# Layer 1 of a two-layer network: folded convolution weights replaced by one projection and shifted rows through DRAM

## The chip, the cores and the metric

The kernel runs on one core of a Trainium2 chip. The metric is the device time of one execution in microseconds (us); the time of a kernel is the median of its runs. One core has a matrix engine (TensorE, PE), a vector engine (VectorE, DVE), an activation engine (ScalarE, ACT), a general engine (GpSimd, POOL) and SyncE (SP), which here issues all the transfers.

## The reference

4096 tokens of 256 channels pass through two layers, each a mixing step and a feed-forward step, with adaptive layer norms around them. Layer 0 is attention with 16 heads and a mixture of experts. Layer 1 is a gated delta rule with four heads of 64 and a "fractal mixer", then a quantized linear step. Only layer 1's first half changes:

```python
def short_conv(x, w):                 # w: 4 taps per channel
    y = sum((xp[:, t:t + l, :] * w[:, t] for t in range(K)))   # xp: 3 zero rows ahead
    return y * jax.nn.sigmoid(y)
# q, k, v = short_conv(x @ W, conv) for each of Wq, Wk, Wv
def fractal_mixer(x, conv_w):
    out = 2.0 * x
    for i in range(4):                # shifted back by 1, 2, 4, 8 rows
        out = out + x_shift * conv_w[i, :, 0] + x * conv_w[i, :, 1]
```

After that, q and k are turned by rotary angles and normed. Within each chunk of 32 tokens a lower triangular matrix, made of k's products and beta, is inverted, and a scan over the chunks carries a state S of 64x64 for each head.

## The kernel before, in words

The 4096 tokens are 32 tiles of 128, or 8 blocks of four tiles. Layer 0's attention runs first, then its mixture of experts (`mixture`, L764), block by block, with layer 1's weights made meanwhile in small pieces, then `layer1` (L1155).

**Fronts.** `fronts` (L1290) is a generator that goes over the blocks. `project` (L1355) transposes the normed block (`nxn`) to channels on partitions (`hT`), splits it in a high and a low part (`hh`, so that three rounded products stand for an fp32 one) and makes the gates. `convolve` (L1409) makes q, k, v and the mixer of one tile directly from `hh`: the projection and its four taps were folded into one set of weights, `taps`, by `taps_in_weights` (L806), which writes them to a DRAM buffer `td`; eight loads of 864 KB bring them in before layer 1. A tile takes 24 matmuls of 128x512 for q and k (four taps, two halves of the channels, three products), 24 of 384 or 256 columns for v and mixer, and four fp32 products with `far` for the mixer's shifts by 4 and 8 rows; the shifts themselves are offsets in `hh`, which keeps eight columns of the block before. ScalarE applies Silu, VectorE turns q and k (`by`, `rot`, L1454 to L1472) and norms them. Some pieces later `by_channel` (L1534) brings them to channels, and `products` (L1551) makes L, which goes through DRAM (`dL`, then `Ls`, L1577), so that all matrices of a block lie on partitions. `solve` (L1581) inverts them in 31 "columns" of two VectorE instructions each, which `solving` (L1629) lets out a few at a time, and the inverse goes through DRAM into `U` (L1619).

**Backs.** `backs` (L1635) goes over the tiles: `from_inverse` (L1657) multiplies U with v and k; `scan` (L1673) has four chunks, each with products of w and S, VectorE's `ut` (L1695), products of ut and k, and VectorE's new `S` (L1718); `weights`, `outputs` and the linear step follow, and the result is stored.

**Order.** `layer1` runs the fronts alone until the first block is solved, then LEAD more front pieces, and then after each yield of the backs RATE front pieces (LEAD 21, RATE 48/60; 60 yields and 48 pieces make a block of four tiles). `later(n, f)` in `stream` puts a function off by n pieces, and so decides where by_channel, products and the first columns stand. TensorE's and VectorE's instructions are pinned in the order of the program (`mm` L139, `tp`, `dv`, `mma`); the rest is placed by a scheduler. SP issues transfers in order[...]. Results of TensorE turn through four PSUM buffers, `pf` (`f` in the profile); the scan's are `w`.

Of the kernel before, what the change touches and what calls it, by code (L numbers as in the profile page):

```python
# [7 lines left out]
F32 = mybir.dt.float32  # L8
# [9 lines left out]
P = 128  # L18
S = 4096
# [22 lines left out]
LEAD = 21  # L42
RATE = 48 / 60
KEPT = 9

A_N = 4 * 2 * 2 * 512
B_W = {3: 384, 2: 384, 1: 384, 0: 256}
B_AT = {3: A_N, 2: A_N + 4 * 384, 1: A_N + 8 * 384, 0: A_N + 12 * 384}  # L50
W_N = A_N + 12 * 384 + 4 * 256
# [51 lines left out]
class _Net:  # L103
# [660 lines left out]
    def mixture(self):  # L764
        nc, tc = self.nc, self.tc
        with ExitStack() as c:
# [18 lines left out]
            taps = self.taps_in_weights()  # L785
            for b in range(NB):
# [4 lines left out]
                for n, f in enumerate(self.experts(b)):  # L791
                    f()
                    while ahead and slots[-len(ahead)] <= n:
                        ahead.pop(0)()
                    if b and n in (1, 4, 8) and taps:
                        taps.pop(0)()
                nc.sync.dma_start(out=self.xd[b], in_=self.xs.pop(b))
                if b == NB - 2:

                    self.right.close()  # L800
                    self.taps = self.t(
                        self.ctx.enter_context(tc.tile_pool(name="taps", bufs=1, side="right")),
                        [P, W_N],
                        "taps",
                        F32R,
                    )  # L806
                    for at in range(0, W_N, 1728):
                        nc.sync.dma_start(
                            out=self.taps[:, at : at + 1728].bitcast(F32), in_=self.td[:, at : at + 1728]
                        )  # L810
# [6 lines left out]
    def taps_in_weights(self):  # L817


        nc, a, dp = self.nc, self.a, self.dram  # L820
        self.td = td = self.t(dp, [P, W_N], "td")
        taps = self.t(self.mw, [P, 3 * C, 4], "taps")
        wide = self.t(self.mw, [P, 2, 3 * C], "wqkv")
        for i, name in enumerate("qkv"):
            cols = slice(C * i, C * i + C)
            nc.sync.dma_start(
                out=taps[:, cols, :].rearrange("p c t -> p (c t)"),
                in_=a["L1_attn_conv_" + name].rearrange("c t -> (c t)").partition_broadcast(P),
            )
            nc.sync.dma_start(  # L830
                out=wide[:, :, cols], in_=a["L1_attn_W" + name].rearrange("(k p) n -> p k n", p=P)
            )
        fw = self.t(self.mw, [P, 4, 2, 2], "fw")
# [5 lines left out]
        own = self.t(self.mw, [P, 2], "own")  # L839
        self.dv(nc.vector.tensor_tensor(own, fw[:, 0, :, 1], fw[:, 1, :, 1], ALU.add))  # L840
        for i in (2, 3):
            self.dv(nc.vector.tensor_tensor(own, own, fw[:, i, :, 1], ALU.add))
        self.dv(nc.vector.tensor_scalar(own, own, 2.0, None, ALU.add))
        pieces = []

        def kept(full, outs):

            _, n, width = full.shape
            cut = self.t(self.ms, [P, 512], "cut")[:, 0 : n * width].rearrange("p (n w) -> p n w", n=n)
            self.dv(nc.vector.tensor_scalar(cut.bitcast(I32), full.bitcast(I32), HIGH, None, ALU.bitwise_and))  # L850
            self.dv(nc.gpsimd.tensor_tensor(full, full, cut, ALU.subtract))
            for half, of in enumerate((cut, full)):
                for i in range(n):
                    nc.sync.dma_start(out=td[:, outs[half][i] : outs[half][i] + width], in_=of[:, i, :])

        def queries_keys(t, k):
            full = self.t(self.ms, [P, 512], "full").unsqueeze(1)
            self.dv(
                nc.vector.tensor_tensor(full[:, 0], wide[:, k, 0:512], taps[:, 0:512, t], ALU.mult)
            )  # L860
            kept(full, [[512 * (4 * t + 2 * half + k)] for half in range(2)])

        def values(t):
            full = self.t(self.ms, [P, 512], "full").rearrange("p (k n) -> p k n", k=2)
            by = taps[:, 512:768, t].unsqueeze(1).to_broadcast([P, 2, C])
            self.dv(nc.vector.tensor_tensor(full, wide[:, :, 512:768], by, ALU.mult))

            outs = [
                [B_AT[t] + B_W[t] * (2 * half + k) + (P if k == 0 and t else 0) for k in range(2)]
                for half in range(2)  # L870
            ]
            kept(full, outs)

        def mixer(t):
            full = self.t(self.ms, [P, 512], "full")[:, 0:C].rearrange("p (k n) -> p k n", k=2)
            for k in range(2):
                col = own[:, k : k + 1] if t == 3 else fw[:, 2 - t, k, 0:1]
                self.dv(nc.vector.tensor_scalar(full[:, k], self.ident, col, None, ALU.mult))
            kept(full, [[B_AT[t] + B_W[t] * (2 * half + k) + C * k for k in range(2)] for half in range(2)])

        for t in range(4):
            pieces += [lambda t=t, k=k: queries_keys(t, k) for k in range(2)]
            pieces.append(lambda t=t: values(t))
            if t:
                pieces.append(lambda t=t: mixer(t))
        return pieces
# [268 lines left out]
    def layer1(self):  # L1155
        nc, tc, a = self.nc, self.tc, self.a
        with ExitStack() as c:
# [9 lines left out]
            self.hT = self.t(wp, [P, 2, 8 + 512], "hT")  # L1167
            self.hh = self.t(wp, [P, 2, 2, 8 + 512], "hh", F32R)
            nc.gpsimd.memset(self.hT[:, :, 0:8], 0.0)
            nc.gpsimd.memset(self.hh[:, :, :, 0:8].bitcast(F32), 0.0)  # L1170
# [6 lines left out]
            self.tiles, self.blocks, self.solved, self.columns = {}, {}, 0, []  # L1177

            front, back = self.stream(self.fronts), self.stream(self.backs)
            def alone(b):  # L1180
                while self.solved < b + 1:
                    next(front, None)
                    self.solving()
# [37 lines left out]
    def layer1_weights(self):  # L1221
# [18 lines left out]
        fw = self.t(wp, [P, 2, 2], "fw")  # L1240
        for i in range(2):
            nc.sync.dma_start(
                out=fw[:, i, :],
                in_=a["L1_attn_frac_conv_w"][2 + i, :, 0].rearrange("(k p) -> p k", p=P),
            )
        w["far"] = self.t(wp, [P, 2, 2, P], "far")
        for i in range(2):
            for k in range(2):
                nc.vector.tensor_scalar(w["far"][:, i, k, :], self.ident, fw[:, i, k : k + 1], None, ALU.mult)


# [38 lines left out]
    def fronts(self, later):  # L1290
        nc = self.nc
        for f in self.norm_block(0):
            f()
        for b in range(NB):
            yield from self.project(b, later)
            for s in range(4):
                if s == 2 and b + 1 < NB:
                    self.load_block(b + 1)
                    for k, f in enumerate(self.norm_block(b + 1)):
                        later(4 + 2 * k, f, quiet=True)  # L1300
                yield from self.convolve(b, s, later)
                n = 4 * b + s
                later(4, lambda n=n: self.by_channel(n))
                later(6, lambda n=n: self.products(n, later))
# [611 lines left out]
```

## Time and profile before

| what | value |
|---|---|
| runs | 3083.62, 3067.89, 3074.98 us, median 3074.98 us |
| profiled execution | 3099.04 us, its span 3097.2 us |
| mean granted TensorE clock | 0.924 |
| layer 0's attention and mixture | to about 2156 us of the span |
| first matmul with `U` | 2312.6 us |
| fronts and scan together | 2312 to 2943 us |
| scan alone | 2943 to 3097 us |

A line of the chain or the timeline has the start and the length in us, then the engine, the tile or the instruction, and the number of records (xN); in square brackets stands how long the engine was idle before and what ended that. A line of stretches has each engine's busy time and number of records, then the granted clock of TensorE (1.00 is full), the busy share of the transfer engines and GB/s. An fp32 matmul leaves two records. The row PEclk on the page shows the granted clock in 40 equal slices, in tenths.

### The profile page before, as it was taken

How to read it: one execution, taken by the hardware profiler on the slowest of the kernel's cores; microseconds unless marked ns; L12 is line 12 of the kernel's file. 1: busy time of each engine (PE TensorE's matmuls, PEld its weight loads, DVE VectorE, ACT ScalarE, POOL GpSimd, SP SyncE). 2: the span in 40 equal slices, each digit the busy share in tenths (PEclk: the TensorE clock that was granted, in tenths of full speed). 3: DMA queues.
4: the chain of work that ended last, by engine and by line, in shares of the span. 5: the costliest groups of instructions: out<-in, count | busy, mean ns of one | idle time of the engine just before them, and what ended most of it. 6: DMA issues, size and time to landing. Idle time of an engine off the chain costs nothing.

```text
span 3097.2 us, 59936 instructions
## 1 busy us (share of the span) xinstructions
PE 2857.7 (92%) x24005; PEld 1674.7 (54%) x24092; DVE 2255.0 (73%) x3905; ACT 1735.3 (56%) x3684; POOL 477.8 (15%) x708
## 2 busy tenths in 40 slices
PE   7899999999999999999999989998878998899877
PEld 4453444444444444444443477776766776677655
DVE  6685889888888988889875177766357667766765
ACT  3335777777777787787887422221444444444321
POOL 3231000000000000000000022221322333333212
PEclk9896999999999999999999599999889998999955
DMA  5453000030000300001000111113111111111100
GB/s 183 139 181 56 12 12 7 12 52 7 12 12 7 52 7 12 12 19 44 7 2 2 48 38 51 55 45 117 38 20 21 21 23 30 29 22 21 22 17 11
DMA packets 174230, 114.30 MB, mean 37 GB/s; under 512 B 122432, under 2 KB 145216, under 8 KB 173376
## 3 DMA queue, kind: packets, MB, share of 16 engines
q1 hardware_dynamic: 173808, 110.41, 13.6%
q8 instruction: 190, 3.11, 0.4%
q14 instruction: 88, 0.72, 0.1%
q0 software_dynamic: 144, 0.07, 0.0%
HBM read 63.62 MB, written 44.89 MB: 35 GB/s over the span
## 4 chain that ended last, share of the span: by engine, by line
PE 66%; DVE 23%; ACT 5%; issue 3%; DMA 2%; POOL 1%; SPq 1%; DVEq 0%; POOLq 0%; ACTq 0%
PE o L142 17%; PE e L142 13%; PE f L142 10%; DVE mx L611 9%; PE m L142 8%; PE b L1352 6%; PE a L1352 4%; PE w L142 2%; PE ps L1352 2%; DVE step L1599 2%; PE f L1352 2%; ACT e L729 2%; DVE T L1606 1%; DVE by L1454 1%; PE f L1343 1%
## 5 line engine op out<-in xcount | busy, mean ns | idle before, releaser
L729 ACT ACTIVATE e<-e 128x512 f32<-128x512 f32 (+1 forms) x2176 | 1153.2, 583 | 346.6 <-PE e L142 313.3
L611 DVE TENSOR_REDUCE mx<-m 128x2 f32<-128x1024 f32 (+3 forms) x1088 | 1201.7, 1128 | 148.0 <-PE m L142 136.1
L142 PE MATMUL o<-e,vall 128*32 128x256 f32 (+2 forms) x9216 | 710.4, 384 | 6.1 <-ACT ot L706 5.2
L142 PE MATMUL e<-q,kt 50*128 50x512 f32 (+3 forms) x2688 | 581.8, 448 | 1.3 <-ACT e L729 1.2
L142 PE MATMUL m<-kt,q 48*128 48x512 f32 (+3 forms) x2688 | 479.4, 375 | 24.2 <-DVE mx L621 9.0
L142 PEld LDWEIGHTS e<-q,kt 50*128 50x128 f32 x2688 | 253.9, 190 | 448.7 <-issue 263.3
L142 PE MATMUL f<-taps,hh 128*128 128x512 f32 (+2 forms) x1536 | 386.0, 394 | 0.3 <-POOL hh L1374 0.3
L142 PEld LDWEIGHTS o<-e,vall 128*32 128x32 f32 x9216 | 194.0, 110 | 332.5 <-issue 307.5
L142 PEld LDWEIGHTS f<-taps,hh 128*128 128x128 f32 x1536 | 278.3, 201 | 40.8 <-POOL hh L1374 0.7
L142 PEld LDWEIGHTS m<-kt,q 48*128 48x128 f32 x2688 | 249.8, 189 | 90.4 <-issue 38.6
L1352 PE MATMUL b<-w,hid 128*128 128x512 f32 x768 | 204.1, 410 | 0.0
L914 POOL TENSOR_TENSOR full<-full,ga 128x512 f32<-128x512 f32 (+1 forms) x2 | 2.0, 1000 | 1122.2 <-DMA full<-in_L_attn_bo_dram 1109.5
L1690 ACT ACTIVATE gs<-S,gm 128x64 f32<-128x64 f32 x256 | 76.5, 342 | 158.1 <-DVE S L1718 158.0
L1352 PEld LDWEIGHTS b<-w,hid 128*128 128x128 f32 x768 | 146.6, 193 | 33.9 <-ACT hid L893 0.3
L1139 DVE SCALAR_TENSOR_TENSOR x<-b,wd,x 128x256 f32<-128x256 f32 x256 | 123.4, 482 | 55.2 <-PE b L1352 48.0
L621 DVE TENSOR_REDUCE mx<-m 128x8 f32<-128x1024 f32 x64 | 78.4, 1225 | 64.3 <-PE m L142 64.2
L1718 DVE TENSOR_TENSOR S<-gs,w 128x128 f32<-128x128 f32 x128 | 36.6, 286 | 118.4 <-PE w L142 117.9
L142 PE MATMUL w<-S,uw 64*32 64x64 f32 x1024 | 60.4, 245 | 58.5 <-DVE S L1718 57.6
L1695 DVE TENSOR_TENSOR ut<-uw,w 32x256 f32<-32x256 f32 x128 | 53.3, 417 | 76.5 <-PE w L142 74.9
L1352 PE MATMUL a<-hs,kt 128*128 128x512 f32 x384 | 103.6, 408 | 1.3 <-DVE hid L1089 1.3
L1599 DVE TENSOR_TENSOR step<-T,Ls 128x126 f32<-128x126 f32 (+22 forms) x248 | 81.2, 327 | 24.8 <-ACT T L1589 19.4
L142 PE MATMUL w<-ut,kk 32*64 32x64 f32 x1024 | 64.3, 250 | 26.6 <-DVE ut L1695 26.6
(288 smaller groups left out, 3167.1 us busy)
## 6 DMA issues: line engine op xcount, KB each, us to landing
q<-qd SPq DMA_DIRECT2D x128, 96.0 KB
kt<-kd SPq DMA_DIRECT2D x12, 768.0 KB
kd<-high SPq DMA_DIRECT2D x32, 256.0 KB
qd<-high SPq DMA_DIRECT2D x32, 256.0 KB
x<-in_L_attn_x_dram SPq DMA_DIRECT2D x15, 512.0 KB
taps<-td SPq DMA_DIRECT2D x8, 864.0 KB
kd<-full SPq DMA_DIRECT2D x16, 256.0 KB
qd<-full SPq DMA_DIRECT2D x16, 256.0 KB
```

The costliest lines, as they stand in the source:

```text
L142: self.nc.tensor.matmul(out, lhsT, rhs, start=start, stop=True, skip_group_check=skip)
L611: nc.vector.tensor_reduce(mx[:, 2 * pair : 2 * pair + 2, s, col], ps[:, :, at : at + w], AX.X, ALU.max)
L621: nc.vector.tensor_reduce(mx[:, 2 * pair : 2 * pair + 2, :, 0], ps.rearrange("p h (s k) -> p h s k", k=P), AX.X, ALU.max,)
L729: nc.scalar.activation(e[:, 0:at], ps[:, 0:at], AF.Exp)
L1139: nc.vector.scalar_tensor_tensor(x, ps[:, e, :], wd[:, s, n : n + 1], x, ALU.mult, ALU.add)
L1343: self.tc.keep_in_program_order(self.nc.tensor.transpose(out, src, ident))
L1352: self.nc.tensor.matmul(out, lhsT, rhs, start=(k == 0), stop=(k == n - 1))
L1454: nc.vector.tensor_tensor(by[z].rearrange("p (i h) f two -> p i (h f) two", i=2), qk.rearrange("p i h (f two) -> p i (h f) two", two=2), c ...
L1599: nc.vector.tensor_tensor(step[:, 0:m, 0:n], T[:, 0:m, j].unsqueeze(2).to_broadcast([P, m, n]), Ls[:, j + 1 : 32, j].unsqueeze(1).to_broad ...
L1690: nc.scalar.activation(gs[:, pair, :], state[:, pair, :], AF.Identity, scale=gm[:, pair, c : c + 1])
L1695: nc.vector.tensor_tensor(ut[rows].rearrange("p (a b) d -> p a b d", b=2), u[rows].rearrange("p (a b) d -> p a b d", b=2), pw[rows, :, 0:1 ...
L1718: nc.vector.tensor_tensor(self.state, gs, pw[:, 0, 128:256].rearrange("p (a d) -> p a d", d=64), ALU.add)
```

## The change

The projections of q, k and v are computed once per block, by channel (channels on partitions, tokens along the row), and written to DRAM buffers of 256 rows with a head of three zeros (eight for the mixer, whose rows are `hT`). `load_shift` brings half a block (256 tokens) of one kind back as a tile of 1 MB: four transfers, each of 32 partitions and 8 groups of 1 KB, and each read from a different shift. Partition 32 i + c of group g so holds channel 32 g + c shifted by i (by 2^i for the mixer). `convolve` multiplies this by stationary matrices of 128x32 with the taps on four diagonals, one for each group of 32 channels: four products stand side by side in four column groups. The mixer also gets its unshifted part by a 128x128 product. Silu is applied by channel, and `mix` transposes the results back to tokens for each tile and goes on as `convolve` did before. Three buffers of shift tiles turn: once a convolution has been issued, the load of the tile three further on is.

The folding of taps, `td`, its loads, `far` and the kept columns of `hh` go. The weights of the front are made in eight pieces in the last block of the mixture. The order is set anew: front pieces per block 35 rather than 48, LEAD 10, shorter delays for keys, products and the first column, more columns at a time, four buffers for `gm`.

```diff
-LEAD = 21
-RATE = 48 / 60
-KEPT = 9
+LEAD = 10
+RATE = 35 / 60
+KEPT = 10
+KINDS = ("q", "k", "v", "m")
...
-            taps = self.taps_in_weights()
+            self.taps_by_row()
+            pieces = []
...
-                    if b and n in (1, 4, 8) and taps:
-                        taps.pop(0)()
+                    if n % 2 and pieces:
+                        pieces.pop(0)()
...
-                    for at in range(0, W_N, 1728):
...
+                    pieces = self.front_weights()
...
-    def taps_in_weights(self):
...
+    def front_weights(self):
...
+        self.rows_d = {}
+        zero = self.t(fp, [P, 2, 8], "zero")
+        nc.gpsimd.memset(zero, 0.0)
+        for kind in KINDS:
+            ahead = 8 if kind == "m" else 3
+            self.rows_d[kind] = d = self.t(self.dram, [C, ahead + S], "d" + kind)
+            nc.sync.dma_start(
+                out=d[:, 0:ahead].rearrange("(k p) n -> p k n", p=P), in_=zero[:, :, 0:ahead]
+            )
...
+        def projection(i, name):
+            full = self.t(self.ms, [P, 512], "full")
+            wide = full.rearrange("p (k n) -> p k n", k=2)
+            nc.sync.dma_start(out=wide, in_=a["L1_attn_W" + name].rearrange("(k p) n -> p k n", p=P))
+            cut = self.t(self.ms, [P, 512], "cut")
             self.dv(nc.vector.tensor_scalar(cut.bitcast(I32), full.bitcast(I32), HIGH, None, ALU.bitwise_and))
...
+            cols = slice(C * i, C * i + C)
+            two = cut.rearrange("p (k n) -> p k n", k=2)
+            nc.scalar.copy(wqkv[:, 0, :, cols], two)
+            self.dv(nc.gpsimd.tensor_tensor(wqkv[:, 1, :, cols], wide, two, ALU.subtract))
+        def taps(kind):
+            for t in range(4):
+                at = slice(32 * t, 32 * t + 32)
+                row = self.rows_of[kind][at, :, 0 if kind == "m" else t].rearrange("p (g c) -> p g c", c=32)
+                eye = self.ident[at, at].unsqueeze(1).to_broadcast([32, 8, 32])
+                self.dv(nc.vector.tensor_tensor(cw[kind][at], row, eye, ALU.mult))
...
-                    self.solving()
+                    self.solving(3)
...
-        nc = self.nc
         for f in self.norm_block(0):
             f()
+        for k in range(2):
+            yield from self.by_channels(0, k)
+        yield from self.gates(0, later)
+        yield from self.project(0)
         for b in range(NB):
-            yield from self.project(b, later)
+            more = b + 1 < NB
             for s in range(4):
-                if s == 2 and b + 1 < NB:
+                n = 4 * b + s
+                parts = self.mix(b, s, later)
+                for kinds in ("qk", "vm"):
+                    if s in (0, 2):
+                        for kind in kinds:
+                            self.convolve(b, s // 2, kind)
+                            yield None
+                    next(parts)
+                    yield None
+                later(3, lambda n=n: self.keys_by_channel(n))
+                later(4, lambda n=n: self.products(n, later))
+                if s == 1 and more:
                     self.load_block(b + 1)
-                    for k, f in enumerate(self.norm_block(b + 1)):
-                        later(4 + 2 * k, f, quiet=True)
-                yield from self.convolve(b, s, later)
-                n = 4 * b + s
-                later(4, lambda n=n: self.by_channel(n))
-                later(6, lambda n=n: self.products(n, later))
-            nc.gpsimd.tensor_copy(self.hT[:, :, 0:8], self.hT[:, :, 512:520])
-            nc.gpsimd.tensor_copy(self.hh[:, :, :, 0:8], self.hh[:, :, :, 512:520])
+                    for at, f in zip((1, 2, 3, 5), self.norm_block(b + 1)):
+                        later(at, f, quiet=True)
+                if s == 2 and more:
+                    for k in range(2):
+                        yield from self.by_channels(b + 1, k)
+            if more:
+                yield from self.gates(b + 1, later)
+                yield from self.project(b + 1)
...
+    def load_shifts(self):
+        while self.loaded < min(self.convolved + 3, self.projected_to):
+            self.load_shift(*divmod(self.loaded // 4, 2), KINDS[self.loaded % 4])
+            self.loaded += 1
+    def load_shift(self, b, h, kind):
+        xs = self.t(self.fx, [P, 8, 256], "shifts")
+        self.shifts[kind] = xs
+        rows = self.rows_d[kind].rearrange("(g c) n -> c g n", c=32)
+        for i in range(4):
+            at = 512 * b + 256 * h + (8 - 2**i if kind == "m" else i)
+            self.nc.sync.dma_start(out=xs[32 * i : 32 * i + 32], in_=rows[:, :, at : at + 256])
...
+    def by_channels(self, b, k):
...
+        at = 8 + 512 * b
+        nc.sync.dma_start(out=self.rows_d["m"][k * P : (k + 1) * P, at : at + 512], in_=hT[:, k])
...
+    def project(self, b):
+        nc = self.nc
+        halves = ((0, 0), (0, 1), (1, 0))
+        for i, kind in enumerate("qkv"):
+            for ch in range(2):
+                ps = self.t(self.pf, [P, 512], "f")
+                cols = slice(C * i + P * ch, C * i + P * ch + P)
+                for n, (k, (wi, hi)) in enumerate((k, z) for k in range(2) for z in halves):
+                    self.mma(ps, self.wqkv[:, wi, k, cols], self.hh[:, hi, k], n, 6)
+                pT = self.t(self.sp, [P, 512], "pT")
+                nc.scalar.copy(pT, ps)
+                at = 3 + 512 * b
+                nc.sync.dma_start(out=self.rows_d[kind][P * ch : P * ch + P, at : at + 512], in_=pT)
+                if ch:
+                    self.projected_to = 8 * b + (8 if kind == "v" else i + 1)
+                    self.load_shifts()
+                yield None
+    def convolve(self, b, h, kind):
+        nc = self.nc
+        xs, cw = self.shifts[kind], self.cw[kind]
+        ps = self.t(self.pf, [P, 2, 256], "f")
+        for k in range(2):
+            if kind == "m":
+                self.mm(ps[:, k], self.own[:, k], self.hT[:, k, 256 * h : 256 * h + 256], skip=True)
+            for g in range(4):
+                n = 4 * k + g
+                self.mm(ps[32 * g : 32 * g + 32, k], cw[:, n], xs[:, n], start=kind != "m", skip=True)
+        self.conv[kind] = out = self.t(self.fp, [P, 2, 256], "conv" + kind)
+        if kind == "m":
+            nc.scalar.copy(out, ps)
+        else:
+            nc.scalar.activation(out, ps, AF.Silu)
+        self.convolved += 1
+        self.load_shifts()
+    def mix(self, b, s, later):
...
         pqk = self.t(self.pf, [P, 2, C], "f")
-        for t in range(4):
+        for i, kind in enumerate("qk"):
             for k in range(2):
-                for wi, hi in halves:
-                    at = 512 * (4 * t + 2 * wi + k)
-                    self.mm(
-                        pqk.rearrange("p i c -> p (i c)"),
-                        shifted(hi, k, t),
-                        self.taps[:, at : at + 512],
-                        start=(t == 0 and k == 0 and (wi, hi) == (0, 0)),
-                        skip=True,
-                    )
-            if t < 3:
-                yield None
+                self.tp(pqk[:, i, P * k : P * k + P], self.conv[kind][:, k, at], self.ident)
         qk = self.t(sp, [P, 2, 4, 64], "qk", bufs=1)
-        nc.scalar.activation(qk.rearrange("p i h d -> p (i h d)"), pqk.rearrange("p i c -> p (i c)"), AF.Silu)
+        nc.scalar.copy(qk.rearrange("p i h d -> p (i h d)"), pqk.rearrange("p i c -> p (i c)"))
...
+        pvm = self.t(self.pf, [P, 2, C], "f")
+        for i, kind in enumerate("vm"):
...
+                self.tp(pvm[:, i, P * k : P * k + P], self.conv[kind][:, k, at], self.ident)
...
-        later(8, begin, quiet=True)
+        later(4, begin, quiet=True)
...
-            self.solving(3)
+            self.solving(4)
...
-            self.solving()
+            self.solving(3)
```

## The prediction

> **What bounds the kernel now.** I read the page's busy shares and its row of granted clock, then a table of stretches, then the chain of waits inside one block of the stage that is changed, then TensorE's timeline there.
>
> ```profile
> PE 2857.7 (92%) x24005; PEld 1674.7 (54%) x24092; DVE 2255.0 (73%) x3905; ACT 1735.3 (56%) x3684; POOL 477.8 (15%) x708
> ...
> PEclk9896999999999999999999599999889998999955
> ```
>
> A share over the whole span decides nothing here: layer 1 begins at about 2156 us. The stretches (PE, PEld, DVE, ACT and POOL busy, granted clock, DMA share, GB/s):
>
> ```profile
> 2230.00:2310.00 80.00, 61.84 (x324) 52.66 (x323) 38.18 (x107) 38.88 (x109) 28.50 (x57) 0.86 0.14 20
> 2415.50:2520.20 104.70, 93.18 (x852) 73.62 (x852) 71.75 (x203) 47.72 (x143) 35.42 (x66) 0.94 0.14 25
> 2943.00:3097.00 154.00, 112.78 (x1070) 80.88 (x1070) 92.25 (x279) 30.77 (x96) 30.79 (x46) 0.54 0.06 14
> 1700.00:1740.00 40.00, 40.00 (x236) 11.33 (x232) 0.00 (x0) 24.96 (x47) 0.00 (x0) 0.50 0.00 1
> 2990.00:3005.60 15.60, 14.55 (x139) 10.65 (x138) 8.35 (x25) 3.86 (x12) 3.27 (x5) 0.50 0.07 16
> ```
>
> So layer 1 has fronts alone to 2312 us (first matmul with U at 2312.6), then 24 tiles of fronts and scan together to 2943 at 26.3 us a tile (a block of four takes 105 us, TensorE busy 93, VectorE 72), then a tail of scans that the change doesn't touch: 154 us. In the middle TensorE is nearly full, but the chain alternates:
>
> ```profile
> 2547.07 3.02 PE f L142 x22
> 2550.30 1.44 PE f L142 x6
> 2552.45 1.25 DVE by L1454 x2
> ...
> 2559.71 0.70 DVE T L1606
> ...
> 2567.72 2.58 PE f L142 x6
> ```
>
> About 60% of the block's chain is TensorE (36 us the convolution's `f`), about 30% VectorE's columns and turning, which stay. A microsecond saved on TensorE is thus worth less than one.
>
> **What leaves.** One tile's convolution, from TensorE's timeline (start, us, records):
>
> ```profile
> 2194.17 5.82 PE L142 MATMUL f<-taps,hh 128*128 128x512 f32 x24
> ...
> 2200.18 2.35 PE L142 MATMUL f<-taps,hh 128*128 128x384 f32 x12
> ...
> 2203.11 2.03 PE L142 MATMUL f<-taps,hh 128*128 128x384 f32 x12
> ```
>
> 5.66 (start to start) + 2.28 + 1.87 + 0.8 for the four `far` products = 10.6 us, 42.5 us a block. In layer 0's mixture the 15 folding pieces go (VectorE 1.07 to 1.25 us plus a 0.43 us cut each); TensorE is 96% busy there, so I count nothing for it. They are replaced by eight smaller pieces in the last mixture block, some 8 us of VectorE where it is busy 65%: they fit beside TensorE's work, and cost up to 3 us if they don't.
>
> **What comes, per block at full clock.**
> - Projection, 36 matmuls of 128x512 at 0.236 us (the row above): 8.5 us.
> - Convolutions: 64 fp32 products of 32 columns by 256. The nearest row is layer 0's `o`, the same form in four column groups (an fp32 matmul leaves two records, so x8 is four products):
>
> ```profile
> 1001.99 0.64 PE L142 MATMUL o<-e,vall 128*32 128x256 f32 x8
> 1002.56 0.52 PE L142 MATMUL e<-q,kt 50*128 50x512 f32 x2
> ```
>
> 0.57 us for four, so 1.14 for a kind and half block, 9.1 us a block. The trace can't tell whether distinct moving operands keep the four side by side; one behind another they would cost 0.34 to 0.43 each, 22 to 27 us a block. I take 9.1, since `o` is the same shape and form.
> - The mixer's `own`, four 128x128x256 fp32 products: `Wo,oT` shows 0.67 for two, so 1.5 us.
> - 32 transposes back, at 0.11 to 0.13 as `nxn` shows: 3.6 us.
>
> Sum 22.7; TensorE saves 19.8 us a block, 158 us over eight, if the clock holds and every microsecond counted.
>
> ScalarE gains six copies and eight activations of about 0.6 us: 48 to 56 us a block, off the path. VectorE keeps its 72 us. SP issues 40 more transfers a block at 0.43 to 0.5 us: 28 to some 46 of 105 us. A 1 MB shift tile is four transfers of 1 KB rows. Rows of 6.9 KB came at 390 to 420 GB/s, 4 KB ones at 286; a block needs 10.4 MB, so anything above about 105 GB/s hides it. For 1 KB rows no row is near: I bound it by 90 and 290, and take 200, because loads run two tiles ahead; each then takes 5 us plus about 2. At 90 the block would be 115 us. The skill ("DMA: Bandwidth & Descriptors", Rules for kernel authors) says transfers to disjoint partition parts serialize on the same engines, which speaks against the four quarters; a load has 105 / 8 = 13 us of time, so by my rate it costs nothing (7 us), and with the page's fixed 2 us paid four times in a row (8 + 5 = 13 us) it would only just fit.
>
> **Order of issue.** Where front pieces fall from 48 to 35 a block, the tile that completes a block's products now meets its first solving column about two chunks of the scan (11 us) later, where before there were three. The path from L over DRAM to T in the trace:
>
> ```profile
> 2936.69 0.38 ACT L1566 ACTIVATE L<-f,bgs 128x128 f32<-128x128 f32 x1
> ...
> 2947.57 0.22 ACT L1589 COPY T<-Ls 64x16 f32<-64x16 f32 x1 [7.25 <-DMA Ls<-dL]
> ```
>
> ```profile
> 2948.39 0.21 DVE L1599 TENSOR_TENSOR step<-T,Ls 128x31 f32<-128x31 f32 x1 [8.16 <-ACT T L1589]
> ```
>
> 10.5 us: just covered. SP's queue is in order, though, and `Ls`, then `dU`, stand behind row writes (which wait for ScalarE's copy) and shift loads (which wait for the convolution that frees the buffer). If that adds 4 us, VectorE stops at the first column, and behind it ut and S, so the scan. I take 2 us a block, between 0 and 4.
>
> **The clock.** This is what decides the size. In the block at 2415 it is 0.94, and falls to half in short stretches of transposes and scan products. In the tail and in 1700 to 1740 it is 0.50 with TensorE 93 and 100% busy: there it has only scan products, or `e` (50 rows) and `o` (32 columns):
>
> ```profile
> 1709.44 1.08 PE L142 MATMUL o<-e,vall 128*32 128x256 f32 x8
> 1710.45 0.79 PE L142 MATMUL e<-q,kt 50*128 50x512 f32 x2
> ```
>
> The skill ("TensorE: Matmul & The Clock Gate", Part 1) would keep the full clock as long as there is no idle window of about 3.4 us. These rows are busy and at half speed, so the rule alone doesn't hold here. The change takes away most dense 128x128x512 products (42.5 us a block become 8.5) and puts column groups and transposes in their place, with more idle time between. By the rule the block falls to 93.2 - 19.8 = 73.4 us of TensorE. By the tail's rows, at half clock: scan 4 x 14.55 = 58; projection 16, convolutions 16 (1.01 us for four), own 4, transposes 8, other front work about 13; sum 115. Yet layer 0's e, m and o ran at 1.00 for hundreds of microseconds, so narrow products don't by themselves take it down. Between the ends 73 and 115 I take a mean clock of 0.70, nearer to full as dense projections and some of the idle-free stretches remain: about 89 us of TensorE.
>
> **The sum.** On the profiled execution's own 3099.0 us (span 3097.2), which lies 24 us above the median of 3074.98; I take those 24 off at the end.
> - Before the first scan: x's load of block 0 is issued ahead of the masks, 5 to 8 us earlier. From the first transposes at about 2168: projection 18 us, the row write and shift loads to the first convolutions at +34, the block's last keys at +52, products +57, Ls +66, columns and their neighbours +93, U over DRAM +101, first product with U at about 2278 (against 2312.6). -34 us, with -20 to -45 possible.
> - 24 tiles (pieces and rate change together, 35 at 35/60 against 48 at 48/60, so the front ends at about the same tile). TensorE 89, idle 11 as now, 2 for late solving: 102 us a block, 25.4 a tile. 24 x 0.9 = -22 us.
> - Tail: nothing.
>
> -56 us: 3043 on the profiled execution, 3019 on the median; I say 3020. In general the median is 2409 + 24 x (us per tile).
>
> **Rivals.**
> 1. The clock stays at 0.93. For it: 1100 to 1140 us at 1.00 with e, m, o. TensorE 73 us, more VectorE on the chain, 90 to 92 us a block: 22.7 a tile, 2954 us. 18%.
> 2. Slower: the clock falls to half through all of the steady stretch and stays. For it: 1700 to 1740, the tail. Against it: the dense projections in each block. 115 us at the tail's 93% is 124 a block, 31 a tile, 3150 us. It decides from 28.4 us a tile (114 a block), a mean clock under about 0.56. 21%, with a partial fall (29 a tile, 3105) the likelier half.
> 3. The change doesn't do what it says: column groups one after another, 13 to 18 us more a block, which with the milder clock gives 28 to 29 a tile if all of it counts and 26.5 if half is covered: 3045 to 3100. 8%.
> 4. Transfers: shift loads under 105 GB/s or Ls and U late by 8 us a block: TensorE waits for `shifts`, and as its order is pinned the scan's products wait behind the convolution, 26.5 to 28.5 a tile, 3045 to 3093. 10%.
>
> The likeliest, a clock of 0.62 to 0.8 (24 to 27 a tile, 2985 to 3057), has 43%. Measurement of this kernel tells about 0.5%, 15 us, from no change. Faster by more: rival 1 (18), the likeliest less its upper edge (40), the lower ends of rivals 3 and 4 (3): 0.61. Within it: that edge (3), the middle of rivals 3 and 4 (10), the mildest of rival 2 (2): 0.15. Slower: the rest, 0.24. The likeliest case's own range is 2985 to 3057; the range for 8 in 10 reaches into rivals 1 and 2: 2945 to 3125.
>
> **What would show it.** PEclk in the steady blocks (0.70 expected); the eight-product groups of a convolution 1.14 us apart at full clock, 2.0 at half (over 2.7 means one after another); no wait of TensorE for `shifts` above 1 us a block; VectorE's `step` waiting for T by some 2 us a block; first product with U near 2278; blocks of about 102 us; the tail still 154 us. A clock outside 0.62 to 0.8 makes the forecast wrong, up or down; so does a tail that changes.

## The result, and the profile after

The changed kernel takes 3222.26 us (3215.78 to 3242.2, four runs), the one before 3071.43 us in the same comparison: 1.0495 times as long, 95% interval 1.0437 to 1.0554. The prediction said 3020, range 2945 to 3125. The profiled execution after has a span of 3215.4 us. Its page, busy shares and clock:

```profile
PE 2805.0 (87%) x23932; PEld 1561.6 (49%) x23932; DVE 2241.8 (70%) x3889; ACT 1794.4 (56%) x3799; POOL 464.4 (14%) x679
...
PEclk9898999999999999999999999976767767678755
```

TensorE has 53 us less to show in all, at a lower clock in the last third. The table of stretches (PE, PEld, DVE, ACT and POOL busy, granted clock, DMA share, GB/s), with the end of layer 0's attention, the steady stretch of 24 tiles and the tail:

```profile
1700.00:1728.00 28.00, 28.00 (x282) 12.44 (x281) 0.00 (x0) 23.37 (x47) 0.00 (x0) 1.00 0.01 2
...
2293.00:3060.00 767.00, 555.98 (x4976) 379.58 (x4974) 422.26 (x1199) 334.88 (x961) 210.61 (x385) 0.70 0.52 102
...
3060.00:3215.00 155.00, 117.91 (x1126) 85.39 (x1126) 94.02 (x279) 31.39 (x97) 31.40 (x47) 0.54 0.05 13
```

The same stretch of the kernel before:

```profile
2312.00:2943.00 631.00, 560.94 (x5110) 442.86 (x5108) 420.02 (x1188) 281.53 (x852) 203.21 (x381) 0.93 0.13 23
```

TensorE is thus busy as long as before (556 and 561 us), at a clock of 0.70 in place of 0.93, and its idle time in the stretch went from 70 to 211 us. The tail is as it was. The first product with U stands at 2293.2, so the 24 steady tiles take 3215.4 - 155 - 2293 = 767 us: 32.0 a tile, 128 a block, against 26.3 and 105. From the mixture's last product to the first with U it is 183 us (2110 to 2293) against 157 before. In the steady stretch TensorE's longest waits (us in total, times, longest) were before

```profile
PE w L142 <- DVE S L1718: 31.9, 24, 3.1
PE w L142 <- DVE ut L1695: 23.3, 12, 3.6
```

and are now

```profile
PE f L136 <- DMA shifts<-dk: 64.2, 6, 11.5
PE w L136 <- DVE S L1734: 54.1, 40, 5.8
PE f L136 <- DMA shifts<-dm: 18.4, 5, 6.7
PE f L136 <- DMA shifts<-dv: 17.9, 6, 4.1
```

So 100 us of waits for shift tiles are new. They come once a block, and about 11 us each time are for k. TensorE's timeline at one handover, and the chain of waits over it (start, us, what), show how it comes about:

```profile
2584.04 1.94 PE L136 MATMUL f<-shifts,cwk 128*32 128x256 f32 x16 [11.18 <-DMA shifts<-dk]
```

```profile
2579.02 5.42 DMA dv<-pT
...
2588.33 13.21 DMA shifts<-dm
```

The block's projection ends at 2571; its rows must be written, and only then can its loads be issued, one behind another in SP's order, while TensorE's pinned order already stands at the convolution, with the scan's products behind it. While the mixer's load is under way the next q is issued too (2589 to 2598), so three tiles share the transfer engines: it takes 13 us rather than the 7 that I had reckoned.

### The profile page after: what moved, and what is told of

The parts are those of the page before. It is cut to its first block, busy times and chain, and to the rows that moved or that the text cites. A ratio compares the mean times of both kernels' runs of the same rounds, so it can differ in the third digit from the quotient of the medians.

```text
span 3215.4 us, 60228 instructions
## 1 busy us (share of the span) xinstructions
PE 2805.0 (87%) x23932; PEld 1561.6 (49%) x23932; DVE 2241.8 (70%) x3889; ACT 1794.4 (56%) x3799; POOL 464.4 (14%) x679
## 5 line engine op out<-in xcount | busy, mean ns | idle before, releaser
L136 PE MATMUL o<-e,vall 128*32 128x256 f32 (+2 forms) x9216 | 692.5, 375 | 6.2 <-ACT ot L700 5.4
L136 PE MATMUL e<-q,kt 50*128 50x512 f32 (+3 forms) x2688 | 573.1, 438 | 1.3 <-ACT e L723 1.3
L136 PE MATMUL m<-kt,q 48*128 48x512 f32 (+3 forms) x2688 | 478.0, 374 | 18.3 <-DVE mx L615 10.7
L136 PE MATMUL w<-S,uw 64*32 64x64 f32 x1024 | 69.5, 273 | 84.4 <-DVE S L1734 82.8
L136 PEld LDWEIGHTS w<-S,uw 64*32 64x32 f32 x1024 | 43.0, 134 | 124.2 <-DVE S L1734 98.5
L136 PE MATMUL f<-shifts,cwk 128*32 128x256 f32 x256 | 26.6, 554 | 87.8 <-DMA shifts<-dk 87.8
L1347 PE MATMUL f<-hh,wqkv 128*128 128x512 f32 x288 | 92.2, 467 | 0.8 <-ACT L L1582 0.6
```

What stands on the lines that cost most here:

```text
L136: self.nc.tensor.matmul(out, lhsT, rhs, start=start, stop=True, skip_group_check=skip)
L1347: self.nc.tensor.matmul(out, lhsT, rhs, start=(k == 0), stop=(k == n - 1))
```

## The experiments

**Moved earlier.** e1: `project(b + 1)` stands before the last tile of block b.

```diff
                     for k in range(2):
                         yield from self.by_channels(b + 1, k)
+                    yield from self.project(b + 1)
             if more:
                 yield from self.gates(b + 1, later)
-                yield from self.project(b + 1)
```

> The changed kernel with one move: the six projection pieces of block b+1 (with their row writes and first shift loads) stand before the last tile of block b, not after it. All shift buffers are free by then. Theory A (what costs is the way from a block's projection over DRAM back to the first convolution, exposed at every handover because TensorE's order is pinned): TensorE's waits for shifts in the steady stretch fall from 100 us to under 30, the time from 3222 to 3120 to 3150 us. Rival B (the rate of the transfers: 10 MB a block at about 200 GB/s with everything else behind it): the waits only move, time within 30 us of 3222. Rival C (TensorE's granted clock, 0.70 in the steady stretch, decides): the waits go, but the idle time turns up elsewhere, 3170 to 3200.

Measured 3227 us. TensorE's waits for shifts fell from 150 to 81 us in all of layer 1, and the steady stretch by 16 us, but the first product with U came 24 us later, since block 1's projection now stands ahead of block 0's last products. The time is the one that rival B gave, but B had the waits only move, and nearly half of them went. What theory A expected, a gain, did not come: what the stretch won was lost ahead of it.

**Without loads, with half of them.** e2 returns from `load_shift` after three tiles; e3 issues two of the four transfers. Both leave the later rows out: the tiles work with what already lies in the buffers. The main lines of e2:

```diff
+        if self.loaded >= 3:
+            self.shifts[kind] = self.three[self.loaded % 3]
+            return
...
```

> The changed kernel that loads only the first three shift tiles and reuses them (all later shift loads are left out, so q, k, v and mixer are wrong after the first tiles); row writes stay. It bounds what all loads together cost. Theory A and rival B: the 165 us that TensorE waits for shifts go, 3040 to 3075 us, clock in the steady stretch up from 0.70 to at most 0.80. Rival C, first form (the narrow products and transposes hold the clock down by themselves): clock stays at 0.70, time not under 3060. Rival C, second form (the waits pull the clock down): clock above 0.85, time under 3020.

> The changed kernel with only two of the four transfers of each shift load after the first three tiles (shifts 2 and 3, or 4 and 8 for the mixer, are left stale, so results are wrong): half the bytes and half the issues, every wait and every place kept. Theory A (latency of the way through DRAM, of which the transfer itself is 5 of some 20 us): 3180 to 3205. Rival B (rate): about half of what leaving all loads out gives, 3125 to 3150.

Measured 3134 and 3168. All loads together cost 88 us. Leaving out half of the transfers takes 54 of them away; 3168 lies in neither range, but as a share of the 88 it is rival B's case rather than A's. It doesn't show that the bytes are what counts, as half the bytes went together with half of SP's issues. And 63 us stay without any load, which A and B had not expected. In e2 the clock of the steady stretch is 0.66 to 0.80.

In e2's handover the timelines of ScalarE, SP (start, us of issue) and VectorE show the next wait:

```profile
2410.11 1.14 ACT L1586 ACTIVATE L<-f,bgs 128x128 f32<-128x128 f32 x4 [1.59 <-PE f L136]
```

```profile
2423.28 0.34 SPq L1892 DMA_DIRECT2D out_dram<-x  x1
...
2427.22 0.34 SPq L1436 DMA_DIRECT2D dv<-pT  x1
...
2428.21 0.85 SPq L1597 DMA_DIRECT2D Ls<-dL  x2
```

```profile
2433.10 0.21 DVE L1619 TENSOR_TENSOR step<-T,Ls 128x31 f32<-128x31 f32 x1 [10.72 <-DMA Ls<-dL]
```

The last tile's L is ready at 2411.3. Its Ls is issued 17 us later, behind a store of results and behind a row write that waited for ScalarE's copy. VectorE stands 10.7 us at the first column, and S and ut behind it.

**Row writes out of the way.** e5: `nc.scalar.dma_start` for the row writes in place of `nc.sync.dma_start`. e6: no loads, and row writes only for block 0.

> The changed kernel with the row writes (q, k, v and the mixer's hT) issued from ScalarE's queue, right behind the copy that makes them, instead of from SP's; the shift loads stay on SP. In the run without loads, SP still stood for up to 8 us at a time before a row write whose copy wasn't done, with Ls queued behind it, and VectorE waited 86 us for Ls. Theory D (SP's order: Ls and dU stand behind row writes, and VectorE's pinned order carries the wait to S): VectorE's waits for Ls fall from 77 us to under 30, time 3222 to 3150 to 3180 us. Rival (rate and shared transfer engines: Ls is late because bulk is under way): waits stay, time within 20 us of 3222.

> The changed kernel without shift loads after the first three and without row writes after the first block (q, k, v, mixer wrong): SP's queue is then that of the kernel before, the new order and all of TensorE's new work stay. Without loads alone it was 3134. Theory D: the 86 us of VectorE's waits for Ls go to under 25, time 3050 to 3080 us. Rival (the new order itself puts the first column too close behind products, as in the kernel before with the new order, which took 40 us more): waits for Ls above 40 us, 3095 to 3125.

Measured 3204 (3190 to 3247) and 3115. Both give some 19 us, which is at the edge of the noise: the intervals of e5 and of the change meet, and so do those of e6 and e2. Theory D fails in both. In e6 VectorE still waited 63 us for Ls and T. In e5's trace it waited 78 us, as in the change (77), so what e5 gained did not come from there. With almost no DRAM traffic of its own for the convolution the change is 44 us slower than before.

**The new order.** e4 puts the change's delays and column counts on the kernel before; e8 only the counts (four and three), e9 only the delays; e10 takes the counts back in e6, e11 starts e6's columns at 6 rather than 4.

```diff
-            self.solving(3)
+            self.solving(4)
...
-            self.solving()
+            self.solving(3)
```

> The kernel before with the order settings of the change alone: keys after 3 pieces rather than 4, products after 4 rather than 6, first column after 4 rather than 8, four and three columns at a time rather than three and two. All theories: within 15 us of 3071. A rival that puts the loss on the new order of columns and products: over 3100.

> The kernel before, with only the number of columns let out at a time as in the change: four ahead of ut and three ahead of S, rather than three and two (three rather than two in the stretch of fronts alone). The whole new order took 40 us more on the kernel before. Theory F (long runs of columns in VectorE's pinned order hold up ut and S, TensorE stands, and its clock falls): 3095 to 3110. Rival G (columns begin before Ls is there): 3060 to 3080.

> The kernel before, with only the delays of the change: keys after 3, products after 4, first column after 4 pieces, columns at a time as before. Theory F: 3060 to 3080. Rival G (first column meets an Ls that isn't there yet): 3095 to 3110, with VectorE's waits for Ls up by over 20 us.

> The changed kernel without shift loads and row writes (as e6: 3115 us, wrong q, k, v and mixer), but three and two columns at a time as in the kernel before. Theory F: 3065 to 3090, clock of the steady stretch up from 0.73 to over 0.78. Rival G: 3105 to 3125.

> The changed kernel without shift loads and row writes (as e6: 3115 us), the first column two pieces later (6 rather than 4), four and three columns at a time as in the change. Rival G: VectorE's 63 us of waits for Ls under 15, 3060 to 3090. Theory F: waits for Ls go, time 3100 to 3125.

Measured: e4 3108 (over 3100, the rival's case), e8 3128, e9 3070 (0.9971 times the kernel before, 0.9933 to 1.0009), e10 3124, e11 3105. On the kernel before, more columns at a time cost over 50 us (F holds, G doesn't); in the changed kernel taking them back gains nothing (F falls there), and beginning later gains 10. The two don't add up: which wait is covered depends on what else TensorE has to do.

**Dense filler for the clock.** e7 puts four dense products ahead of each convolution in e6. e12, e13 and e15 put four, half as wide, into the scan, ahead of the `w` products, in the kernel before, in e11's kernel and in e14's; e14 is the whole change with e5's and e11's edits.

```diff
+    def filler(self):
+        for n in range(4):
+            self.mma(self.w2[:, 1, 256:512], self.taps[:, 0:P], self.taps[:, 0:256], n, 4)
...
+            self.filler()
             for pair in range(2):
```

> The same without rows and loads, plus four dense 128x128x512 products ahead of each convolution, whose result is overwritten: 32 a block, 7.5 us of TensorE at full clock, pure extra work. If the clock falls because dense products are gone (my reading in the prediction): clock in the steady stretch up by over 0.1 against the run without the filler, time no longer or shorter. If the clock follows TensorE's idle time: clock within 0.05, time longer by 30 to 70 us.

> The kernel before with four dense 128x128x256 products (0.12 us each at full clock) ahead of each of the scan's eight product groups of a tile, written to a part of the scan's PSUM tile that nothing reads: pure extra work, 3.8 us of TensorE a tile at full clock, and able to run while TensorE waits for VectorE. Theory H (the clock falls after a wait of some 2 to 3 us and comes back only when dense products run; scan products and transposes alone don't bring it back): clock of the tail from 0.54 to over 0.85, the tail from 154 to 130 to 150 us, all in all 3030 to 3080. Rival I (density doesn't matter): tail clock under 0.65, tail longer by 30 to 60 us, total over 3120.

> The changed kernel without shift loads and row writes and with the first column at 6 (as e11: 3105 us, clock of the steady stretch 0.73 to 0.80), with the same filler in the scan. Theory H: clock over 0.90 in the steady stretch and the tail, time down to 3030 to 3075 although TensorE has 15 us more work a block. Rival I: clock within 0.05, time 3140 or more.

> The whole change, nothing left out, with the two orders that helped: row writes on ScalarE's queue (alone 3204) and the first column at 6 pieces rather than 4 (10 us without DRAM). 3180 to 3200 if the two add up; the shift loads' share and the clock stay.

> The same with the filler in the scan. Theory H: clock of the steady stretch from about 0.70 to over 0.85, time 3110 to 3160, still behind the kernel before, as the shift loads stay. Rival I: over 3230.

Measured: 3132, 3159, 3159, 3240, 3292. The tail of e12 and of e13, against 0.54 without filler:

```profile
3000.00:3166.00 166.00, 136.57 (x1310) 105.57 (x1310) 91.56 (x275) 30.35 (x94) 30.92 (x46) 0.74 0.05 12
```

```profile
3017.00:3171.00 154.00, 123.83 (x1326) 95.41 (x1325) 87.21 (x257) 30.73 (x95) 31.62 (x47) 0.83 0.05 13
```

So the filler does bring the clock up: on the clock H has the direction (0.54 to 0.74 and 0.83 in the tails, less than it said; 0.84 to 0.87 in most of e13's steady stretch, against 0.73 to 0.80), I has not. On the time it is the other way round: H's are wrong in all three, and the totals that I gave hold. The filler costs more than the clock gives back (four of its products take 0.67 us at full clock in e12's tail, where I had reckoned 0.48), so it says nothing of what a higher clock alone would gain. Nor does it show that the dense form is what counts: it also fills waits (TensorE's for S in the tail went from 25.7 to 18.4 us in e12), and no run put narrow products in its place. e7 lies between its two cases: clock up by some 0.06, 17 us longer.

e14 shows that e5's and e11's gains don't add: 3240, against 3204 for e5. VectorE's waits for Ls and T did go, from 77 us to 12, without a gain: TensorE's waits for S and ut grew from 60 to 86 us in the steady stretch, and those for shift tiles fell only from 100 to 81. So the late Ls of e2's handover is a wait that can be seen, but removing it was worth nothing here.

**Why less work brought so little.** e17 leaves the convolution out: it replaces the 68 convolution products a block of e6 (64 in column groups and the mixer's four dense ones, not 16) by eight rounded ones:

```diff
-            for g in range(4):
...
+        self.mm(ps.rearrange("p k n -> p (k n)"), self.wqkv[:, 0, 0, 0:P], self.hh[:, 0, 0])
```

> The changed kernel without shift loads and row writes (as e6: 3115 us), with the 64 column-group products and the mixer's 16 dense ones of a block replaced by eight rounded products of 128x128x512 (convolution left out): 9 us a block of TensorE less at full clock, some 16 at half. If TensorE's work still bounds the steady stretch: down by 50 to 90, 3025 to 3065. If the chain between TensorE and VectorE in the scan bounds it (S and ut waiting on each other, with less left to fill in): under 25 us, 3090 to 3115.

Measured 3082, 33 us under e6, between the two cases. Of these, some 15 lie before the first product with U (137 us after the mixture, 152 in e6) and some 14 behind it. The steady stretch of e6 and of e17:

```profile
2485.00:2600.00 115.00, 95.06 (x815) 65.17 (x814) 69.29 (x197) 55.17 (x155) 36.41 (x67) 0.69 0.12 23
```

```profile
2490.00:2605.00 115.00, 89.34 (x736) 65.24 (x736) 73.21 (x209) 57.05 (x163) 37.34 (x68) 0.66 0.12 23
```

Nine microseconds of work (at full clock) less a block, and TensorE is busy nearly as long as before, at a lower clock; it waits 92 us for S and 32 for ut. Behind the first scan the work taken away was worth about a fifth of its size.

**The transfers.** e16: from block 4 on, rows of 8 KB rather than 1 KB in the same four transfers. e18: from there one transfer onto all 128 partitions in place of four. What they load is as large as the shifted rows, but isn't these rows. e18's edit:

```diff
+        if b >= 4:
+            self.nc.sync.dma_start(
+                out=xs.rearrange("p g n -> p (g n)"),
+                in_=self.rows_d[kind][0:P, 512 * (b - 3) : 512 * (b - 3) + 2048],
+            )
+            return
```

> The whole change, but from block 4 on each shift load reads rows of 8 KB that lie together (the same four transfers, partitions and bytes, other data: q, k, v and mixer wrong from there), so blocks 0 to 3 and 4 to 7 differ in nothing but the length of a row. Rate by row length: a 256 KB transfer in blocks 4 to 7 at nearly twice the rate, TensorE's waits for shifts there under half of those of blocks 1 to 3, 3165 to 3195 us. Rival (fixed latency and place in the queue): waits as before, 3210 to 3230.

> The whole change, but from block 4 on each shift tile comes in one transfer of 128 partitions and 8 KB rows, in place of four of 32 partitions (the same bytes, other data: q, k, v and mixer wrong from there). With four transfers of 8 KB rows the rate stayed at 220 to 229 GB/s, against 205 to 210 with 1 KB rows. If 32 partitions are what limits the rate: 380 to 430 GB/s in blocks 4 to 7, TensorE's waits for shifts there under 15 us, 3160 to 3180 us. If not: 210 to 240 GB/s, 3185 to 3200 us, as with long rows.

Measured 3193 and 3169. The rate of transfers in 40 slices, over 80 us of the change, 80 us of e16 and 60 us of e18 (GB/s; where the rate stays level, the transfer engines are busy for 80% of the time or more):

```profile
GB/s 131 0 133 72 37 185 197 233 239 2 75 58 157 149 213 202 14 200 216 197 185 183 224 207 212 249 206 212 204 208 209 37 0 8 78 169 154 190 69 33
```

```profile
GB/s 227 217 203 170 173 75 150 202 203 240 131 225 225 221 229 225 217 234 209 217 291 217 234 90 0 0 0 213 225 86 0 136 28 33 34 36 36 10 66 0
```

```profile
GB/s 37 0 0 88 1 0 0 19 24 56 44 0 5 94 81 175 0 11 0 5 41 145 339 382 265 79 246 379 260 169 81 220 366 426 415 421 393 344 300 350
```

Where it stays level, in the second half of the first line, 32 partitions at a time give mostly 204 to 212 GB/s; with 8 KB rows it is mostly 209 to 234; one transfer of 128 partitions gives 366 to 426. TensorE's waits for shifts from 2600 to 3000 us fell from 58 to 31 us in e16 and to 10.5 in e18, and the kernels won 29 and 53 us. e18 thus has the rate, the waits and the time of its first case.

Not all of this is the rate. e16 gained its 29 us at nearly the old rate, which neither of its cases had. Both edits changed one thing more: from block 4 on they read only the first 128 channels, that is, only what the first of a kind's two row writes brings. SP's queue at a handover of the change and of e16:

```profile
2572.12 0.34 SPq L1432 DMA_DIRECT2D dv<-pT  x1
...
2579.02 0.45 SPq L1432 DMA_DIRECT2D dv<-pT  x1
2584.50 2.31 SPq L1363 DMA_DIRECT2D shifts<-dv  x4
```

```profile
2696.34 2.51 SPq L1439 DMA_DIRECT2D dv<-pT  x2
2701.26 1.71 SPq L1367 DMA_DIRECT2D shifts<-dv  x4
```

In the change the second row write of v stands behind k's loads, and v's load waits for it to land. From v's first row write to v's first load it takes 11.8 to 12.9 us in the change, but 4.5 to 5.6 in the last four blocks of e16 and 2.5 to 4.5 in those of e18. These 7 us a block, 28 in four blocks (an estimate from these issue times), are as much as e16's whole gain. What is left for one transfer in place of four is then the 24 us between e16 and e18. Whether the partitions or the number of transfers set the rate no run separates. Loads of 864 KB onto 128 partitions, several one behind another, ran at 390 to 420 GB/s in the kernel before, which speaks for the partitions.

## Why the prediction was wrong, step by step

- **What comes and leaves on TensorE: right in size.** Eight column-group products take 1.07 us at full clock and 1.94 at half (forecast 1.14 and 2.0), so they do run side by side, and rival 3 is out.
- **The clock: right in size, with a wrong proof, so in part by luck.** The mean of the steady stretch is 0.70, as forecast. But the row at 1700 to 1740 that I used says nothing of `e` and `o`: in the trace after, they run at 1.00 there (first row of the stretches). The half clock there came and went from one execution to the next. Of the 20 profiled ones it stands at this place in e14 too (28 of 28 us busy at 0.50, 1700 to 1728), and earlier in the attention, around 1450 us, in e5 and e13. In the execution before it made the attention end at 1757 rather than 1728 us, and so accounts for the 24 us that I took off at the end. What the traces do show, change first, then before:

```profile
2454.00:2464.00 10.00, 0.85 (x4) 0.39 (x3) 2.33 (x10) 1.75 (x6) 0.72 (x1) 0.69 0.82 153
...
2468.00:2470.00 2.00, 1.25 (x18) 0.83 (x16) 1.83 (x9) 1.71 (x5) 0.79 (x2) 0.99 1.06 221
...
2504.00:2522.00 18.00, 17.08 (x144) 10.95 (x142) 9.74 (x28) 8.54 (x27) 6.54 (x10) 0.50 0.19 28
```

```profile
2478.00:2482.00 4.00, 0.87 (x10) 0.47 (x10) 3.66 (x11) 1.77 (x5) 1.18 (x2) 1.00 0.20 41
2482.00:2486.00 4.00, 3.56 (x17) 3.26 (x18) 3.80 (x14) 0.59 (x2) 0.80 (x2) 0.58 0.13 9
2486.00:2490.00 4.00, 4.00 (x36) 3.38 (x35) 2.54 (x10) 2.18 (x8) 3.11 (x7) 0.99 0.59 108
```

  Behind a wait of TensorE (9.9 us in the change, 3.6 before) the clock is at half in both kernels. In both it is back after some 4 us of work, before under dense products of 384 and 256 columns, in the change under column groups and transposes. But behind two shorter waits (1.7 and 0.6 us, up to 2502) the change's clock fell again and stayed at half for 18 us that were 95% busy with scan products, transposes and column groups. So what ends such a stretch these rows don't settle, and the filler, which also fills waits, doesn't either.
- **TensorE's 89 us a block: nearly right.** 556 of 767 us is 93 a block of 128.
- **Idle "11 as now, 2 for late solving": this is the step that failed.** It is 35, not 13. Of the 211 idle us of the steady stretch TensorE waits 100 for shift tiles, which I had put at nothing, and 54 for S, against 32 before. Why the waits for S grew is argued and not shown: before, there was nearly always a front product to fill the time, and the change takes many of these away. Late solving I priced at 2 us a block, between 0 and 4; VectorE's waits for Ls and T were 77 us in all, about 10 a block, but by e14 this was not what the time hung on.
- **"So by my rate it costs nothing": failed.** The rate was right (200 forecast, 204 to 212 measured), the cover was not. I set 5 + 2 us against an even 13 us per load, but the first loads of a block can't start before its rows are written, and then three share the transfer engines. All loads cost 88 us; leaving the row writes out as well (e6) gives 19 more.
- **The Trainium skill's rule against the four quarters** ("DMA: Bandwidth & Descriptors", Rules for kernel authors: one 128-partition transfer rather than parts). I set my own rate of 200 GB/s against it. e18 bears the rule out, at twice the rate and up to 24 us for four of the eight blocks; I had looked for the price in four fixed costs of 2 us, which the page (section "Anatomy of one DMA") gives for transfers issued by GpSimd, while here SP issues them.
- **Before the first scan**: 34 us gain forecast; from the mixture's end it is 26 us longer. In e2, without loads, it is 153 us, four less than before. So the loads cost 30 us there, where the fronts run alone and no scan covers them. The mixture, counted at nothing, became 16 us shorter from its first to its last step (398 to 382).
- **The tail: right**, 154 and 155 us.
- **The rivals.** Rival 4 (transfers, Ls and U late) comes nearest: TensorE waits for `shifts` and the scan's products wait behind. It had 10% and was too cheap, 26.5 to 28.5 us a tile against 32.0, and the rate under 105 GB/s that it asked for wasn't the reason. Rival 2 (half clock throughout) is not what happened, and neither is rival 1 (the clock stays at 0.93): the mean was 0.70.

The account by the medians: 151 us = 88 for shift loads + 19 for row writes + 44 that stay without either. Layer 0's attention, which no edit touches, ends between 1726 and 1772 us in the profiled executions, so differences of some 20 us between medians are weak. From the mixture's last product on, the profiled executions give much the same: 163 us = 90 + 17 + 56. What the 44 consist of is settled only in part: in the steady stretch of e6, taking more work from TensorE is worth a fifth of its size (e17), a low clock and the waits for S and ut stand there together, and no run separated one from the other. No version of the change beat the kernel before; e9, the kernel before with the change's delays, equals it.

## What to carry to other kernels

Work that goes through DRAM and back needs a place in the order where its whole way, write, load and the queue it stands in, lies beside other work; a mean rate says nothing about the first load of a burst. In a kernel where a serial chain alternates between two engines, the busy engine's other work is the cover of the chain, and taking it away can shorten little. A wait in a trace has its price only by the run without it: here one of 77 us went, and nothing was gained. Load a tile onto all 128 partitions at once, and don't take one stretch of one execution for a rule on the clock: another execution ran the same instructions at full clock.

## What the runs showed of the hardware

- Four transfers onto 32 partitions each: mostly 204 to 212 GB/s with 1 KB rows and mostly 209 to 234 with 8 KB rows; one onto 128 partitions 366 to 426. The length of the row made under a tenth.
- TensorE's clock at 0.50 through 18 us in which it was 95% busy, and at 0.99 some 4 us after a wait of 9.9 us; extra products in the scan took the tail's clock from 0.54 to 0.74 and 0.83.
- The same instructions of the attention, 100% busy, at 0.50 in one execution and at 1.00 in another.
